# Sums of an LSTM's input blocks moved ahead of the other stream on GpSimd, and the copies of three-token blocks dropped

## The chip, the cores and the metric

The kernel runs on one core of a Trainium2 chip. The metric is the device time of one execution in microseconds (us), the median over several runs. In the profile PE is TensorE's matrix multiplication, PEld its loading of weights, DVE is VectorE, ACT is ScalarE, POOL is GpSimd, and SP is SyncE, from which most DMAs are issued. "L1154" is line 1154 of the kernel's source.

## The reference

Four residual layers work on x of shape 128 x 64 x 256 (batch, tokens, channels), in fp32, each on a layer-normalized and rectified input: a graph convolution with batch normalization, a graph network with LSTMs, attention over the graph, and attention with four heads. The change lies in the second layer. There h, after two graph convolutions, goes through four LSTMs one after the other:

```python
for p in range(1, MAX_SKIP + 1):
    nw = Tv // p
    wins = h[:, :nw * p, :].reshape(Bv * nw, p, Hd)
    last = _lstm_last(Wih[p - 1], Whh[p - 1], bih[p - 1], bhh[p - 1], wins)
    idx = jnp.arange(nw) * p + (p - 1)
    h = h.at[:, idx, :].set(last.reshape(Bv, nw, Hd))
```

LSTM p takes windows of p tokens, runs p steps with its own weights (`g = x_t @ Wih.T + h @ Whh.T + bias`, gates i, f, g, o from zero states) and writes the last state over the last token of each window. LSTM p + 1 reads the result. With 64 tokens there are 64, 32, 21 and 16 windows per batch entry for p = 1, 2, 3, 4.

## The kernel before

The batch is cut into 16 chunks of 512 rows (8 batch entries of 64 tokens). Layer 2 takes two chunks at a time in eight passes, numbered 0 to 7. A pass holds h in a tile `hT`, channels on the partitions in two halves k, and in the free dimension token t and batch entry b (16 of them). An LSTM of p tokens thus has nw x 16 columns: 1024, 512, 336 and 256.

**Seven products instead of eight.** The product of a gate's weights with a step's columns is taken as a product of 2 x 2 blocks: two halves of the channels by two halves of the columns. It is done with seven block products, numbered 1 to 7, in place of eight. Products 1, 2 and 3 take blocks of the tokens as they are. Products 5, 6, 7 and 4 take sums of blocks, which `differences` makes in four subtractions (L313, L314, L315, L316): t1 = b12 − b11, t3 = b22 − b12, t2 = b22 − t1, t4 = b21 − t2. For the input part x these sums are made on GpSimd into the tile `xd`, a pool of two buffers; for the state part h they are made on VectorE into `hd`. Products of x and h add up in the same PSUM bank; the pool has two banks each of the tags x, y and z.

**Three tokens.** The columns are cut in halves by window for p = 2 and 4, so that a block is rows of 16 contiguous values. 21 windows are odd, so for p = 3 the cut is by batch entry: a block is 21 rows of 8 values. In that case `operands_x` (L1086) also copies the blocks of products 1, 2 and 3 into `xd` (L1097), three copies of 128 x 168 on GpSimd for each step but the first, behind the four sums.

**One LSTM's start** (`lstm`, L1026): `operands_x(1)` is the first thing it emits. The first step has no state; its 12 products g (L1125) read `hT` directly into the six banks (two with tag y for gate i, two with z for gate g, two with x for gate o), and ScalarE makes the gates from them (`first_acts`, L1112), freeing the banks in the order y, z, x. Then, before the state of the first step is there, come the x parts of the second step's products 5 (bank y), 3 and 2 (bank z), L1154. The state h and its sums follow on VectorE, and then the rest of the products. At the last step `new_state` writes into `hT` (L1079, L1083).

**The single-token LSTM** (`single`, L1278) has its whole work in seven products of 512 columns with three gates each (L1308). It makes its sums at its own start for passes 1 to 7, the first (t1) on VectorE and the other three on GpSimd. In pass 0 it makes them after its first yield.

**The other stream.** The LSTMs are generators, and at each of their yields, numbered n = 0 to 21 in a pass, the kernel emits pieces of other work, given by lists of places such as `CONV`, `BEGUN`, `RESIDUAL` and `AHEAD`: the graph convolutions of the next pass, the way back of the previous pass's result, and the normalization ahead of layer 3. The order in which all this is emitted is the order on each engine's queue. An LSTM yields a last time at its end: n = 3, 7, 13 and 21 for p = 1 to 4. Pieces that stand there are emitted before the next LSTM's `operands_x(1)`. At n = 3 and n = 7 these are layer-norm statistics: four pairs of bn_stats and bn_aggr on VectorE (L159, L160), then the reciprocal root rstd on GpSimd (`rsqrt`, L99 and L100), which waits for them. Of those at n = 3 the scale and shift follow at n = 4 (nmr, L194, on VectorE; four applications on ScalarE, L196), ahead of that LSTM's first gates on ScalarE. Only in pass 0 does n = 21 have a piece of VectorE's, the addition of line 284.

Of the kernel before, what the change touches and what calls it, by code (L numbers as in the profile page):

```python
# [8 lines left out]
F32 = mybir.dt.float32  # L9
# [4 lines left out]
P = 128  # L14
# [5 lines left out]
def kernel(  # L20
# [22 lines left out]
    nc = tc.nc  # L43
    B, T, D = x.shape
    H0 = w1t.shape[1]
    KD = D // P
# [3 lines left out]
    SKIP = wih_t.shape[0]  # L50
    HEADS = 4
    HD = D // HEADS
    CH = 512
    NJ = CH // P
    NB = CH // T
    NCH = B * T // CH
    SUP = 2
# [11 lines left out]
    def pool(name, bufs, side="left"):  # L69


        stack = ExitStack()
        return stack.enter_context(tc.tile_pool(name=name, bufs=bufs, side=side,
                                                reuse_waits="tile")), stack.close
# [234 lines left out]
    def differences(engine, dst, b11, b12, b21, b22, third=None):  # L309


        t1, t2, t3, t4 = dst
        return [lambda: engine.tensor_tensor(t1, b12, b11, OP.subtract),  # L313
                lambda: ((third or engine).tensor_tensor(t3, b22, b12, OP.subtract),  # L314
                         engine.tensor_tensor(t2, b22, t1, OP.subtract)),  # L315
                lambda: engine.tensor_tensor(t4, b21, t2, OP.subtract)]  # L316
# [272 lines left out]
    with tc.manual_schedule(engines={mybir.EngineType.PE, mybir.EngineType.DVE,  # L589
# [27 lines left out]
        for c in range(2, NCH - 1):  # L617
            a, z = sevens[c], sevens.get(c - 1)
# [3 lines left out]
            b = sevens[c + 1] = Seven1(c + 1) if c + 1 < NCH - 1 else None  # L622
# [142 lines left out]
    with tc.manual_schedule(engines={mybir.EngineType.PE, mybir.EngineType.DVE,  # L765
# [3 lines left out]
        for c in range(2, NCH - 1):  # L769
            a, b, z = sevens[c], sevens.get(c + 1), sevens.get(c - 1)  # L770
# [80 lines left out]
    l1, close_l1 = pool("l1", 2)  # L851
# [31 lines left out]
    def load_sets(n):  # L883
        for _ in range(min(n, len(coming))):
            p, q = coming.pop(0)
            wsets[p, q] = w1.tile([P, 15, P], F32, tag="wset", name=f"wset_{p}_{q}", bufs=6)
            nc.sync.dma_start(wsets[p, q], wfar[p, q])
# [4 lines left out]
    hTs = {}  # L892
# [130 lines left out]

    BLOCKS = {1: (0, 8), 2: (2, 9), 3: (7, 14), 4: (3, 10), 5: (4, 11), 6: (5, 12), 7: (6, 13)}

    def lstm(p, hv, name, follows):  # L1026


        nb = hv.shape[3]
        nw = hv.shape[2] // p  # L1030
        n = nb * nw
        m = n // 2
        bs = bias[:, p - 1, :]
        odd = nw % 2
        inner = nb // 2 if odd else nb

        def cols(s):
            return slice(s, s + (nw - 1) * p + 1, p)

        def tokens(k, s, j):  # L1040
            v = hv[:, k, cols(s), :]
            if odd:
                return v[:, :, j * inner : (j + 1) * inner]
            return v[:, j * nw // 2 : (j + 1) * nw // 2, :]

        def folded(t):
            return t.rearrange("p (a b) -> p a b", b=inner)
# [35 lines left out]
                engine.tensor_tensor(tokens(c, s, j), folded(gate(3, c, part)),  # L1083
                                     folded(gate(2, c, part)), OP.mult)

        def operands_x(s):  # L1086

            t = l1.tile([P, 7 * (T // 3) * NB], F32, tag="xd", name=f"xd_{name}_{s}", bufs=2)
            t = [folded(t[:, i * m : (i + 1) * m]) for i in range(7 if odd else 4)]
            b = {(k, j): tokens(k, s, j) for k in range(KD) for j in range(2)}  # L1090
            for f in differences(nc.gpsimd, t[:4], b[0, 0], b[0, 1], b[1, 0], b[1, 1]):
                f()
            o = dict(zip((5, 6, 7, 4), t))
            for i, (kind, kj) in enumerate(((1, (0, 0)), (2, (1, 0)), (3, (1, 1)))):
                if odd:

                    nc.gpsimd.tensor_copy(t[4 + i], b[kj])  # L1097
                o[kind] = t[4 + i] if odd else b[kj]
            return o

        b = {(k, j): hn[:, k, halves[j]] for k in range(KD) for j in range(2)}
        dh = differences(nc.vector, [hd[:, i, :m] for i in range(4)], b[0, 0], b[0, 1], b[1, 0], b[1, 1])
        oh = {i: folded(a) for i, a in {1: b[0, 0], 2: b[1, 0], 3: b[1, 1], 4: hd[:, 3, :m],
                                        5: hd[:, 0, :m], 6: hd[:, 1, :m], 7: hd[:, 2, :m]}.items()}
        ox = {1: operands_x(1)}

        banks = {(q, c): bank(f"g{q}_{name}_{c}", tag) for q, tag in ((0, "y"), (2, "z"), (3, "x"))
                 for c in range(KD)}
# [76 lines left out]
        def each(us, *fs):  # L1185
            for f in fs:
                for u in us:
                    f(u)
# [4 lines left out]
        def do(f, *a):  # L1193
            return lambda u: getattr(u, f)(*a)
# [4 lines left out]
        for s in range(1, p):  # L1199
            last = s == p - 1  # L1200
            B = [Unit(q, s) for q in (1, 3)]
            if not last:
                ox[s + 1] = operands_x(s + 1)
            each(A, pe(5, "h"), do("copy", 5), pe(1), do("copy", 1), pe(3, "h"), pe(6, "x"), pe(6, "h"),
                 pe(2, "h"), do("u4"), do("c11"), do("c12"))
            each(B, pe(5), do("copy", 5))
            each(A, do("act", 0), pe(7), do("c22"), do("act", 1))
            each(B[:1], pe(3), pe(2))
            each(A, pe(4), do("act", 2))
            if last:  # L1210
                load_sets(2)
            nc.gpsimd.tensor_mul(gates[:, 0, :, :n], gates[:, 0, :, :n], gates[:, 2, :, :n])  # L1212
            each(B[1:], pe(3), pe(2))
            each(B, pe(1), do("copy", 1))
            yield
            each(B, pe(6))
            A = [] if last else [Unit(q, s + 1) for q in (0, 2)]
            each(A, pe(5, "x"))

            def cell(c, part):  # L1220
                nc.vector.tensor_mul(cells[:, c, part], cells[:, c, part], gate(1, c, part))
                nc.vector.tensor_add(cells[:, c, part], cells[:, c, part], gate(0, c, part))  # L1222
                nc.scalar.activation(gate(2, c, part), cells[:, c, part], AF.Tanh)  # L1223

            if last:

                each(B[:1], do("u4"), do("c11"), pe(7))
                each(B[1:], do("u4"), pe(7))
                each(B[:1], do("c22"), do("c12"), do("act", 0))
                each(B[1:], do("c22"), do("c11"), do("c12"), do("act", 0))  # L1230
                cell(0, every)
            else:
                for u in B:
                    each([u], do("u4"), do("c11"), do("c12"), do("act", 0))
                cell(0, every)
                each(B, pe(7), do("c22"))
            each(B, do("act", 1))
            each(A[:1], pe(3, "x"), pe(2, "x"))
            new_state(s, 0, every)
            if not last:  # L1240
                dh[0]()
            each(A[1:], pe(3, "x"), pe(2, "x"))
            each(B, pe(4))
            B[0].act(2)
            cell(1, halves[1])
            B[1].act(2)
            cell(1, halves[0])
            new_state(s, 1, halves[1])
            if not last:
                dh[1]()  # L1250
            new_state(s, 1, halves[0], nc.gpsimd if follows and last else nc.vector)
            if last:
                load_sets(2)
            else:
                dh[2]()
            yield
# [18 lines left out]

    KINDS1 = {1: 0, 2: 1, 4: 2, 5: 3, 6: 4, 7: 5, 3: 6}

    def single(b, name, begun):  # L1278

        m = CH
        wide = b[0, 0].shape[1:]
# [5 lines left out]
        def folded(a):  # L1289
            return a.rearrange("p (a b) -> p a b", b=wide[1]) if len(wide) > 1 else a  # L1290
# [1 line left out]
        def at(g, c, j):  # L1292
            return (more if j else cells)[:, c, :m] if g == 2 else gates[:, 2 * g + j, c, :m]

        t = []
        for i in range(2):
            part = l1.tile([P, 7 * (T // 3) * NB], F32, tag="xd", name=f"xd_{name}_{i}", bufs=2)
            t += [folded(part[:, a : a + m]) for a in range(0, 2 * m, m)]
        right = {1: b[0, 0], 2: b[1, 0], 3: b[1, 1], 4: t[3], 5: t[0], 6: t[1], 7: t[2]}
        ys, xs_ = [[bank(f"{n}_{name}_{g}", tag) for g, tag in enumerate(tags)]  # L1300
                   for n, tags in (("y1", "yyz"), ("x1", "zxx"))]

# [20 lines left out]
        def state(c, j):  # L1323
            nc.vector.tensor_mul(b[c, j], folded(at(2, c, j)), folded(at(0, c, j)))

        def copy(dst, kind):
            for g in range(3):
                nc.scalar.copy(at(g, *dst), ps(g, kind))
# [2 lines left out]
            for g in range(3):  # L1331
                nc.vector.tensor_add(at(g, *dst), at(g, *dst), ps(g, kind))

        first = differences(nc.vector, t, b[0, 0], b[0, 1], b[1, 0], b[1, 1])[:1]
        rest = differences(nc.gpsimd, t, b[0, 0], b[0, 1], b[1, 0], b[1, 1])[1:]
        if begun:
            for f in first + rest:
                f()
        product(2)
        copy((0, 0), 2)  # L1340
        if not begun:
            yield
            for f in first + rest:
                f()
        product(1)
        add((0, 0), 1)
        for g in range(3):
# [31 lines left out]
        tanh(1, 0)  # L1379
        state(1, 1)  # L1380
        state(1, 0)
        yield

    def lstms(sc, hT):
        hv = hT.rearrange("p k (t b) -> p k t b", t=T)

        def tokens(k, j):
            if sc:
                return hv[:, k, j * T // 2 : (j + 1) * T // 2, :].rearrange("p t b -> p (t b)")
            return hv[:, k, :, j * NB : (j + 1) * NB]  # L1390

        yield from single({(k, j): tokens(k, j) for k in range(KD) for j in range(2)}, f"{sc}_1", sc > 0)
        for p in range(2, SKIP + 1):
            yield from lstm(p, hv, f"{sc}_{p}", p == SKIP and sc < NCH // SUP - 1)

    def new_hT(sc):

# [654 lines left out]
```

## Time and profile before

| | before |
|---|---|
| median of 3 runs | 1901.11 us (1900.84 to 1902.15) |
| span of the profiled execution | 1897.3 us |
| layer 2's LSTM passes in it | about 279 to 1520 us, a middle pass about 157.4 us |
| GpSimd copies of three-token blocks (L1097) | 48, of 0.31 to 0.60 us |
| GpSimd sums, 128 / 168 / 256 / 512 columns | from 0.45 / 0.53 / 0.72 / 1.26 us each |

The table's last two rows are the durations of the instructions themselves[...]. A line of a timeline has the start, the duration, the engine, the source line, the operation, out<-in, the shape, the number of merged instructions, and in brackets how long the engine stood idle before it and which instruction released it. Every TensorE product appears as two matmuls, so that 12 products g are "x24".

### The profile page before, as it was taken

To read this page: it belongs to the slowest core of one execution; us is meant where nothing else is said; L and a number is where in the kernel's file an instruction comes from. 1 tells how busy PE (TensorE), PEld (TensorE's weight loads), DVE (VectorE), ACT (ScalarE), POOL (GpSimd) and SP (SyncE) were. 2 spreads that over 40 slices of the span, in tenths; PEclk is the share of its full clock that TensorE was granted. 3 is DMA by queue.
4 is the path that set the end of the run, shared out by engine and by line. 5 is a ranking of instruction groups with operands and counts; after the bars stand their busy time and mean duration, and the time that the engine had idled before them with its cause. 6 is when DMAs were issued, how large, how long until landed. Compare 5 with 4: busy or idle time off the path is not lost.

```text
span 1897.3 us, 39092 instructions
## 1 busy us (share of the span) xinstructions
PE 1862.9 (98%) x15077; PEld 1478.2 (78%) x15077; DVE 1238.9 (65%) x3150; ACT 1015.9 (54%) x2284; POOL 569.7 (30%) x752
## 2 busy tenths in 40 slices
PE   8999989999999999999999999999999999999998
PEld 6877856895896798689589679868969967777776
DVE  6768746566576666667657666665565567677776
ACT  5766544556456446555645645655565544444453
POOL 5856621212221322222322231222122213233232
PEclk9999999999999999999999999999999999999999
DMA  3223643225334433333433443333144345444433
GB/s 114 78 68 149 232 168 109 72 88 184 106 129 145 144 128 129 113 119 115 150 117 129 150 139 137 130 109 106 54 150 139 103 134 157 135 139 152 143 114 113
DMA packets 111273, 241.45 MB, mean 127 GB/s; under 512 B 11504, under 2 KB 74864, under 8 KB 111088
## 3 DMA queue, kind: packets, MB, share of 16 engines
q1 hardware_dynamic: 110192, 237.09, 37.1%
q8 instruction: 119, 1.95, 0.4%
q0 software_dynamic: 320, 1.05, 0.2%
q10 hardware_dynamic: 576, 0.82, 0.1%
q14 instruction: 66, 0.54, 0.1%
HBM read 170.50 MB, written 68.42 MB: 126 GB/s over the span
## 4 chain that ended last, share of the span: by engine, by line
PE 86%; DVE 7%; POOL 3%; ACT 2%; issue 1%; DMA 0%; DVEq 0%; SPq 0%; ACTq 0%
PE x L1154 22%; PE z L1154 11%; PE g L1125 7%; PE v L1542 6%; PE y L1154 5%; PE x L1308 4%; PE y L1308 3%; PE p_q L1549 3%; PE v L915 3%; PE X L1738 3%; PE X L423 2%; PE X L499 2%; PE u L929 2%; PE Y L1738 1%; PE Y L423 1%
## 5 line engine op out<-in xcount | busy, mean ns | idle before, releaser
L1163 DVE TENSOR_TENSOR gates<-gates,x 128x128 f32<-128x128 f32 (+2 forms) x384 | 118.3, 320 | 332.1 <-PE x L1154 324.9
L1154 PE MATMUL x<-xd,wset 128*128 128x128 f32 (+2 forms) x1280 | 285.6, 311 | 0.7 <-DVE gates L1163 0.2
L1154 PE MATMUL x<-hd,wset 128*128 128x128 f32 (+2 forms) x1152 | 246.7, 303 | 0.0
L1212 POOL TENSOR_TENSOR gates<-gates 128x512 f32<-128x512 f32 (+2 forms) x48 | 74.9, 1560 | 521.7 <-ACT gates L1068 521.7
L1154 PEld LDWEIGHTS x<-xd,wset 128*128 128x128 f32 x1280 | 202.1, 190 | 19.1 <-DVE gates L1163 6.1
L1068 ACT ACTIVATE gates<-gates,bias 128x256 f32<-128x256 f32 (+4 forms) x384 | 170.4, 490 | 56.2 <-DVE gates L1163 52.8
L1154 PEld LDWEIGHTS x<-hd,wset 128*128 128x128 f32 x1152 | 185.1, 191 | 5.0
L1125 PE MATMUL g<-hT,wset 128*128 128x256 f32 (+2 forms) x576 | 183.9, 474 | 1.1 <-DVE hT L1079 1.1
L1160 ACT COPY gates<-y 128x128 f32<-128x128 f32 (+2 forms) x192 | 54.2, 293 | 212.9 <-PE y L1154 212.4
L1125 PEld LDWEIGHTS g<-hT,wset 128*128 128x128 f32 x576 | 108.6, 190 | 69.7 <-issue 38.5
L1154 PE MATMUL z<-hs,wset 128*128 128x128 f32 (+2 forms) x768 | 154.0, 303 | 0.0
L1154 PEld LDWEIGHTS z<-hs,wset 128*128 128x128 f32 x768 | 119.8, 191 | 3.3
L1160 ACT COPY gates<-x 128x128 f32<-128x128 f32 (+2 forms) x192 | 56.4, 295 | 93.7 <-PE x L1154 92.9
L1163 DVE TENSOR_TENSOR gates<-gates,z 128x128 f32<-128x128 f32 (+2 forms) x384 | 104.3, 315 | 0.1
L1068 ACT ACTIVATE gates<-x,bias 128x128 f32<-128x128 f32 (+2 forms) x192 | 74.7, 389 | 49.4 <-PE x L1154 46.5
L1154 PE MATMUL z<-hT,wset 128*128 128x128 f32 (+1 forms) x512 | 97.1, 302 | 0.0
L1112 ACT ACTIVATE gates<-g,bias 128x512 f32<-128x512 f32 (+2 forms) x144 | 74.5, 559 | 32.1 <-PE g L1125 31.6
L1154 PE MATMUL x<-hs,wset 128*128 128x128 f32 (+2 forms) x384 | 84.8, 303 | 0.0
L1223 ACT ACTIVATE gates<-cell 128x256 f32<-128x256 f32 (+2 forms) x144 | 55.2, 384 | 50.5 <-DVE cell L1222 49.0
L1154 PE MATMUL y<-xd,wset 128*128 128x128 f32 (+2 forms) x384 | 77.4, 304 | 3.4 <-ACT gates L1112 3.4
L1154 PE MATMUL y<-hd,wset 128*128 128x128 f32 (+2 forms) x384 | 80.1, 311 | 0.0
L1154 PEld LDWEIGHTS z<-hT,wset 128*128 128x128 f32 x512 | 76.7, 191 | 3.9 <-ACT gates L1112 0.6
(329 smaller groups left out, 4211.5 us busy)
## 6 DMA issues: line engine op xcount, KB each, us to landing
wset<-wfar SPq DMA_DIRECT2D x96, 960.0 KB, 6.6
hT<-far_h SPq DMA_DIRECT2D x124, 128.0 KB, 3.1
far_h<-hm SPq DMA_DIRECT2D x16, 512.0 KB, 3.0
far_n<-xs SPq DMA_DIRECT2D x16, 512.0 KB, 3.3
xs<-far_n SPq DMA_DIRECT2D x64, 128.0 KB, 4.2
far_x<-xs SPq DMA_DIRECT2D x16, 512.0 KB, 3.0
x<-far_x SPq DMA_DIRECT2D x64, 128.0 KB, 3.2
xt<-in_x_dram SPq DMA_DIRECT2D x15, 512.0 KB, 4.1
```

The lines of the kernel that those rows point to most:

```text
L423: nc.tensor.matmul(self.banks[tag][:, i * CH // 2 : (i + 1) * CH // 2], w, self.at[kind], start=first and not i, stop=True, skip_group_che ...
L915: nc.tensor.matmul(banks[m], wg0_sb[:, k, m * P : (m + 1) * P], agg[:, k, :], start=(k == 0), stop=(k == KD - 1))
L1068: nc.scalar.activation(gate(q, c, part), src, AF.Tanh if q == 2 else AF.Sigmoid, bias=bs[:, q * KD + c : q * KD + c + 1])
L1112: nc.scalar.activation(columns_of(gate(q, c)), natural(banks[q, c][:, :n].rearrange("p (w b) -> p w b", b=nb)), AF.Tanh if q == 2 else AF. ...
L1125: nc.tensor.matmul(banks[q, c][:, :n].rearrange("p (w b) -> p w b", b=nb), wsets[p, q][:, 2 * k + c, :], hv[:, k, : (nw - 1) * p + 1 : p, ...
L1154: nc.tensor.matmul(folded(self.psum(kind)), wsets[p, self.q][:, BLOCKS[kind][i], :], (ox[self.s] if part == "x" else oh)[kind], start=firs ...
L1160: nc.scalar.copy(gate(self.q, kind // 5, halves[kind // 5]), self.psum(kind))
L1163: nc.vector.tensor_add(gate(self.q, *dst), gate(self.q, *a), self.psum(kind))
L1212: nc.gpsimd.tensor_mul(gates[:, 0, :, :n], gates[:, 0, :, :n], gates[:, 2, :, :n])
L1308: nc.tensor.matmul(folded(ps(g, kind)), wih1[:, g, KINDS1[kind], :], right[kind], start=kind in (2, 5, 1), stop=True, skip_group_check=True)
L1542: nc.tensor.matmul(ps[:, i, :], hT[:, k, j, :], w[:, k, first : first + D], start=(k == 0), stop=(k == KD - 1))
L1738: nc.tensor.matmul(st[c, tag][:, i * CH // 2 : (i + 1) * CH // 2].rearrange("p (a n) -> p a n", n=P), w, st[c, "o7"][kind], start=first an ...
```

## The change

The sums of an LSTM's input blocks leave the start of `lstm` and `single`. A function `ending`, called at the end of each LSTM just before its last yield, makes those for the next LSTM: `operands_x(p + 1, ..., 1)` for the next p, or `block_sums` of the next pass's tile after p = 4. So they come ahead of whatever the other stream puts at that yield, on GpSimd and, for t1 of the single-token LSTM, on VectorE. The copies for p = 3 are dropped: products 1, 2 and 3 read their blocks in `hT`, as they do for p = 2 and 4. Sums for later steps of an LSTM stay where they were.

The purpose is that the sums start as soon as the tokens they need are written, and that nothing is copied that TensorE can read in place.

```diff
+    def operands_x(p, hv, name, s):
+        nw, nb, inner, tokens = columns_x(p, hv)
+        m = nw * nb // 2
+        t = l1.tile([P, 7 * (T // 3) * NB], F32, tag="xd", name=f"xd_{name}_{s}", bufs=2)
+        t = [t[:, i * m : (i + 1) * m].rearrange("p (a b) -> p a b", b=inner) for i in range(4)]
+        b = {(k, j): tokens(k, s, j) for k in range(KD) for j in range(2)}
+        for f in differences(nc.gpsimd, t, b[0, 0], b[0, 1], b[1, 0], b[1, 1]):
+            f()
+        return {5: t[0], 6: t[1], 7: t[2], 4: t[3], 1: b[0, 0], 2: b[1, 0], 3: b[1, 1]}
...
-            for i, (kind, kj) in enumerate(((1, (0, 0)), (2, (1, 0)), (3, (1, 1)))):
-                if odd:
-
-                    nc.gpsimd.tensor_copy(t[4 + i], b[kj])
-                o[kind] = t[4 + i] if odd else b[kj]
...
-        ox = {1: operands_x(1)}
+        ox = {1: x1}
...
             if last:
                 load_sets(2)
+                ending()
...
-        if begun:
-            for f in first + rest:
-                f()
         product(2)
         copy((0, 0), 2)
+        begun = bool(t)
         if not begun:
             yield
-            for f in first + rest:
-                f()
+            t = block_sums(b, name)
...
+        def ending(p):
+
+            if p < SKIP:
+                operands[p + 1] = operands_x(p + 1, hv, names[p + 1], 1)
+            elif sc < NCH // SUP - 1:
+                nxt = hTs[sc + 1].rearrange("p k (t b) -> p k t b", t=T)
+                operands[1] = block_sums(blocks(sc + 1, nxt), f"{sc + 1}_1")
```

More of the change, by code (lines that the diff above doesn't have):

```diff
@@ L1024, with columns_x, tokens, lstm @@
     BLOCKS = {1: (0, 8), 2: (2, 9), 3: (7, 14), 4: (3, 10), 5: (4, 11), 6: (5, 12), 7: (6, 13)}
-    def lstm(p, hv, name, follows):
-        nb = hv.shape[3]
-        nw = hv.shape[2] // p
+    def columns_x(p, hv):
+        nw, nb = hv.shape[2] // p, hv.shape[3]
+        odd = nw % 2
+        inner = nb // 2 if odd else nb
+        def tokens(k, s, j):
+            v = hv[:, k, s : s + (nw - 1) * p + 1 : p, :]
+            if odd:
+                return v[:, :, j * inner : (j + 1) * inner]
+            return v[:, j * nw // 2 : (j + 1) * nw // 2, :]
+        return nw, nb, inner, tokens
+    def operands_x(p, hv, name, s):
[7 more added lines that the diff above has]
+        return {5: t[0], 6: t[1], 7: t[2], 4: t[3], 1: b[0, 0], 2: b[1, 0], 3: b[1, 1]}
+    def lstm(p, hv, name, follows, x1, ending):
+        nw, nb, inner, tokens = columns_x(p, hv)
         n = nb * nw
@@ L1034, in lstm @@
         odd = nw % 2
-        inner = nb // 2 if odd else nb
         def cols(s):
             return slice(s, s + (nw - 1) * p + 1, p)
-        def tokens(k, s, j):
-            v = hv[:, k, cols(s), :]
-            if odd:
-                return v[:, :, j * inner : (j + 1) * inner]
-            return v[:, j * nw // 2 : (j + 1) * nw // 2, :]
         def folded(t):
@@ L1084, in new_state @@
                                      folded(gate(2, c, part)), OP.mult)
[L1086 to L1091, printed above, removed]
-                f()
-            o = dict(zip((5, 6, 7, 4), t))
-            for i, (kind, kj) in enumerate(((1, (0, 0)), (2, (1, 0)), (3, (1, 1)))):
-                if odd:
-                    nc.gpsimd.tensor_copy(t[4 + i], b[kj])
-                o[kind] = t[4 + i] if odd else b[kj]
-            return o
         b = {(k, j): hn[:, k, halves[j]] for k in range(KD) for j in range(2)}
@@ L1202, in lstm @@
             if not last:
-                ox[s + 1] = operands_x(s + 1)
+                ox[s + 1] = operands_x(p, hv, name, s + 1)
             each(A, pe(5, "h"), do("copy", 5), pe(1), do("copy", 1), pe(3, "h"), pe(6, "x"), pe(6, "h"),
@@ L1276, with blocks, tokens, block_sums @@
     KINDS1 = {1: 0, 2: 1, 4: 2, 5: 3, 6: 4, 7: 5, 3: 6}
-    def single(b, name, begun):
+    def blocks(sc, hv):
+        def tokens(k, j):
+            if sc:
+                return hv[:, k, j * T // 2 : (j + 1) * T // 2, :].rearrange("p t b -> p (t b)")
+            return hv[:, k, :, j * NB : (j + 1) * NB]
+        return {(k, j): tokens(k, j) for k in range(KD) for j in range(2)}
+    def block_sums(b, name):
+        t = []
+        for i in range(2):
+            part = l1.tile([P, 7 * (T // 3) * NB], F32, tag="xd", name=f"xd_{name}_{i}", bufs=2)
+            for a in range(0, 2 * CH, CH):
+                v = part[:, a : a + CH]
+                wide = b[0, 0].shape[1:]
+                t.append(v.rearrange("p (a b) -> p a b", b=wide[1]) if len(wide) > 1 else v)
+        a = b[0, 0], b[0, 1], b[1, 0], b[1, 1]
+        for f in differences(nc.vector, t, *a)[:1] + differences(nc.gpsimd, t, *a)[1:]:
+            f()
+        return t
+    def single(b, name, t, ending):
         m = CH
@@ L1293, in at @@
             return (more if j else cells)[:, c, :m] if g == 2 else gates[:, 2 * g + j, c, :m]
[L1295 to L1299, printed above, removed]
+        right = {1: b[0, 0], 2: b[1, 0], 3: b[1, 1]}
         ys, xs_ = [[bank(f"{n}_{name}_{g}", tag) for g, tag in enumerate(tags)]
@@ L1332, in add @@
                 nc.vector.tensor_add(at(g, *dst), at(g, *dst), ps(g, kind))
-        first = differences(nc.vector, t, b[0, 0], b[0, 1], b[1, 0], b[1, 1])[:1]
-        rest = differences(nc.gpsimd, t, b[0, 0], b[0, 1], b[1, 0], b[1, 1])[1:]
-        if begun:
-            for f in first + rest:
-                f()
         product(2)
         copy((0, 0), 2)
+        begun = bool(t)
         if not begun:
             yield
-            for f in first + rest:
-                f()
+            t = block_sums(b, name)
+        right.update(zip((5, 6, 7, 4), t))
         product(1)
@@ L1381, in single @@
         state(1, 0)
+        ending()
         yield
+    operands = {}
     def lstms(sc, hT):
         hv = hT.rearrange("p k (t b) -> p k t b", t=T)
[L1387 to L1392, printed above, removed]
+        names = [f"{sc}_{p}" for p in range(SKIP + 1)]
+        def ending(p):
[4 more added lines that the diff above has]
+                operands[1] = block_sums(blocks(sc + 1, nxt), f"{sc + 1}_1")
+        yield from single(blocks(sc, hv), names[1], operands.pop(1, None), lambda: ending(1))
         for p in range(2, SKIP + 1):
-            yield from lstm(p, hv, f"{sc}_{p}", p == SKIP and sc < NCH // SUP - 1)
+            yield from lstm(p, hv, names[p], p == SKIP and sc < NCH // SUP - 1, operands.pop(p),
+                            lambda: ending(p))
     def new_hT(sc):
```

## The prediction

> **What bounds the kernel now.** I read the page first, then TensorE's own waits, then the order of time around them.
>
> ```profile
> span 1897.3 us, 39092 instructions
> PE 1862.9 (98%) x15077; PEld 1478.2 (78%) x15077; DVE 1238.9 (65%) x3150; ACT 1015.9 (54%) x2284; POOL 569.7 (30%) x752
> ...
> PE 86%; DVE 7%; POOL 3%; ACT 2%; issue 1%; DMA 0%; DVEq 0%; SPq 0%; ACTq 0%
> ```
>
> TensorE is busy 98% of the span, so work taken from GpSimd brings nothing by itself; only the moments at which TensorE stands still count. The view of its waits lists them:
>
> ```profile
> PE z L1154 <- POOL xd L1097: 9.5, 6, 1.7
> PE y L1154 <- ACT gates L1112: 3.4, 3, 2.3
> ...
> PE y L1308 <- DVE xd L313: 0.9, 1, 0.9
> ```
>
> (total us, times, longest.) The longest total is a wait for the copies of line 1097, exactly what the change deletes: six times, 1.7 us at most. Six suggests once in most of the eight passes. The order of time at the start of the three-token LSTM of pass 2, TensorE first (weight loads apart; start, duration), then GpSimd:
>
> ```profile
> 653.85 6.94 PE L1125 MATMUL g<-hT,wset 128*128 128x336 f32 x24
> 660.62 0.73 PE L1154 MATMUL y<-xd,wset 128*128 128x168 f32 x4
> 662.91 1.27 PE L1154 MATMUL z<-xd,wset 128*128 128x168 f32 x7 [1.55 <-POOL xd L1097]
> ```
>
> ```profile
> 657.51 0.23 POOL L99 TENSOR_SCALAR rstd_n<-mv_n 128x4 f32<-128x4 f32 x1 [12.65 <-DVE mv_n L160]
> 657.82 1.04 POOL L100 TENSOR_TENSOR rstd_n<-rstd_n,mhalf 128x4 f32<-128x4 f32 x1
> 658.83 0.54 POOL L313 TENSOR_TENSOR xd<-hT 128x168 f32<-128x168 f32 x1
> 659.33 0.54 POOL L314 TENSOR_TENSOR xd<-hT 128x168 f32<-128x168 f32 x1
> 659.82 0.81 POOL L315 TENSOR_TENSOR xd<-hT,xd 128x168 f32<-128x168 f32 x1
> 660.71 0.68 POOL L316 TENSOR_TENSOR xd<-hT,xd 128x168 f32<-128x168 f32 x1
> 661.34 1.52 POOL L1097 COPY xd<-hT 128x168 f32<-128x168 f32 x3
> ```
>
> VectorE's last write of hT (L1083) runs from 654.86 to 655.28: there the tokens are complete, but GpSimd takes up the other stream's rstd first, and that waits for four statistics on VectorE until 657.5. Sums and copies follow only then. The products y start at 660.62. Four of 168 columns pass at 0.285 us a pair (at 666.02 and 666.30 pairs start 0.28 apart), so the next could start at 661.19; it starts at 662.91. TensorE loses 1.72 us. The same spacing of starts, measured at all eight three-token LSTMs, gives 1.71, 1.72, 1.86, 1.72, 1.72 and 1.72 us in passes 1 to 6: 10.45 us. Pass 0 loses 0.1 there. In pass 7 no rstd stands ahead on GpSimd, the copies are done at 1441.2, and the z products follow y by 0.57 us (1442.81, 1443.38), the bare pace: the trace already holds one LSTM without this wait.
>
> [...] The trace agrees (pairs of 0.45 us start every 0.285), so I count starts. [...] a GpSimd sum of 256 columns takes 0.73 us beside the PSUM copy of line 1005 and 1.27 beside the addition of line 284. [...] In pass 0 the single-token LSTM already reads hT in runs of 8: six products of 512 columns take 2.57 us from one group's start to the next (285.36 to 287.94), as they do from xd (280.21 to 282.79).
>
> **The change part by part.**
>
> *Copies removed*: 6 for each of eight passes, 48 in all, at 0.31 to 0.60 us on GpSimd (line 1097's rows). The z products then need only hT, complete at 655.28, and their banks, which ScalarE's first four gates free at 658.00 + 2.23 = 660.23. TensorE comes at 661.19. So the whole 1.72 us goes: −10.4 us in six passes.
>
> *Does the next wait take it back?* TensorE then reaches y<-hd at 663.6 instead of 665.34. Its hd (VectorE L313) was done at 662.14, the last hs at 662.67, the difference for product 6 at 663.63 while TensorE would ask for it near 666.6; the aggregation between needs a tile that VectorE finished at 658.6. Every one is ready at least 1 us early. Nothing.
>
> *Sums ahead of the other stream*: no instruction is added; on GpSimd the four sums change places with rstd at the ends of the one- and two-token LSTMs. For three tokens: sums from 655.3, 4 x 0.5 = 2.0 us beside one-input statistics, done at 657.4 as rstd's input comes (657.5). Nobody is delayed. Alone this would also have removed the wait: copies of 0.3 each would end at 658.4. The two parts therefore share one gain; it is not counted twice.
>
> *The same for two tokens* is where a new wait could arise, because there the rstd is wanted at once:
>
> ```profile
> 619.11 2.07 ACT L196 ACTIVATE cv<-xs,nmr_b,rstd_b 128x256 f32<-128x256 f32 x4 [4.15 <-DVE nmr_b L194]
> 621.09 1.24 ACT L1112 ACTIVATE gates<-g,bias 128x512 f32<-128x512 f32 x2
> ```
>
> ScalarE applies the other stream's normalization, then makes the first gates; TensorE takes the y banks at 622.78. Tokens are complete at 614.77. Four sums of 256 columns take 4 x 0.70 = 2.8 us alone, 3.9 if two are slowed as in this trace. So rstd starts at 617.7 to 618.8 instead of 617.00 and ends 1.35 later (617.00 to 617.31 + 1.04), at 619.05 to 620.1. nmr waits for it on VectorE; behind nmr is queued the addition of line 284, and ScalarE's four applications wait, then the first gates that free the y banks. Before, nmr ran at 618.93, held by VectorE's copies until 619.0, so ScalarE comes 0.2 to 1.2 us later. The first y bank is free after one gate, at 621.09 + 0.66 = 621.75, 1.0 us before TensorE takes it, the second with 0.8 to spare. I take the lower value, since VectorE runs one-input statistics in that time: no wait. The upper end costs 0.4 us in six passes, 2.4 us.
>
> *Pass 0, two tokens*: here TensorE already waits 2.3 us on those first gates. The sums now start beside the addition of line 284, slow each other, and rstd comes 0.3 to 0.6 later: +0.4 us.
>
> *Single-token sums, pass 0 to 1*: only here another unit stands ahead on VectorE (the addition of line 284, 437.50 to 439.0, and t1 at 438.98, slowed to 1.75 us). Now t1 is first: the 0.9 us wait of y L1308 goes; by starts 1.0. In later passes nothing changes places: 0.
>
> *Strided reads*: 192 products of three tokens now read hT in runs of 8, at 0 by the comparison above. Two semaphores at some x products (GpSimd besides VectorE or ScalarE): both long past, 0.
>
> Sum: −10.4 − 1.0 + 0.4 = −11.0; 1901.1 − 11.0 = 1890.1.
>
> **The rivals.**
>
> B. *The late rstd bites.* ScalarE is held for 1.2 us in six passes, TensorE for 0.4, and pass 0 loses more: 1890.1 + 3 = 1893. For it: the slack is only 0.8 us. Against it: VectorE's statistics leave GpSimd alone.
>
> C. *A wait in place of the one removed*: TensorE comes 1.7 us early to y<-hd or a bank that is not ready, and the gain shrinks to that of the single sums: about 1900. For it: there are many such waits at hundredths of a us. Against it: pass 7 runs without the wait, and nothing stops behind it (y<-hd at 1445.61 comes straight after the filling transposes).
>
> D. *Strided reads slow TensorE.* The 192 products are recorded as 384 matmuls of 0.142 us, 54.5 us. Half as slow again: +27, so 1890.1 + 27 = 1917, slower than before. For it: no product in the trace yet reads runs of 8 that lie three tokens apart. Against it: pass 0's runs of 8 at full pace, and the first products g read hT of three tokens in place, in runs of 16, 336 columns at 0.283 us.
>
> E. *More than counted*: fewer GpSimd operations beside VectorE's shorten its chains, and some of the gaps of about 0.1 us ahead of x<-xd at 168 columns go (by the spacing of starts 53 of them, 5.3 us in all): half of them, 1887.5.
>
> **How the numbers follow.** Forecast 0.68, B 0.17, C 0.07, D 0.05, E 0.03. Time: the forecast's, 1890.1. Range: from E, 1887.5, to B with its upper cost in pass 0 and a part of the gain lost, 1896; C and D, 0.12, are left out. Faster: forecast, B and E, 0.88. Same: C, 0.07. Slower: D, 0.05.
>
> **What would show it.** Right: no z wait for xd on TensorE, z<-hT 0.57 us after y in all passes, y L1308 without its wait, p=3 groups at 168 columns with the mean of 0.306 us and the pace unchanged. B: PE y waiting for ACT gates L1112 near 622 in six passes. C: y<-hd waiting for DVE. D: z<-hT of 168 columns spaced wider than 0.142. The sum is wrong if the span of a middle pass (157.4 us) does not fall by about 1.7.

## The result, and the profile after

| | before | after |
|---|---|---|
| median | 1901.21 us (1900.84 to 1902.15) | 1890.13 us (1889.59 to 1892.57) |
| ratio, with its 95% interval | | 0.9943 (0.9926 to 0.9961) |
| profiled execution, span | 1897.3 us | 1890.8 us |

The change saves 11.1 us by the medians; the interval of the ratio allows 7.4 to 14.1. The page of the changed kernel (first lines, then the chain that ended last by engine):

```profile
span 1890.8 us, 39088 instructions
PE 1863.0 (99%) x15077; PEld 1479.3 (78%) x15077; DVE 1236.6 (65%) x3150; ACT 1016.6 (54%) x2284; POOL 551.4 (29%) x704
...
PE 90%; DVE 5%; ACT 2%; issue 1%; POOL 1%; DMA 1%; SPq 0%; DVEq 0%; ACTq 0%
```

TensorE does the same 15077 matmuls in a span 6.5 us shorter; GpSimd has 48 instructions fewer and has nearly left the chain (3% before, 1% now). The view of TensorE's waits (total us, times, longest), its first lines:

```profile
PE y L1155 <- ACT gates L1113: 3.3, 2, 2.5
PE idle_a L151 <- POOL ident masks.py:199: 2.7, 1, 2.7
PE s L1843 <- issue: 2.3, 2, 1.2
```

The 9.5 us of z waiting for the copies and the 0.9 us of the single-token y waiting for t1 stand nowhere in it. What leads now is pass 0's old wait for the first gates, and a line that hardly counted before (0.4 us): attention products at which TensorE waited for "issue", nothing that the profile names. The start of the three-token LSTM of pass 2, first TensorE in order of time, then GpSimd:

```profile
653.31 6.94 PE L1126 MATMUL g<-hT,wset 128*128 128x336 f32 x24
660.09 0.73 PE L1155 MATMUL y<-xd,wset 128*128 128x168 f32 x4
660.66 1.30 PE L1155 MATMUL z<-hT,wset 128*128 128x168 f32 x8
```

```profile
652.35 0.59 POOL L313 TENSOR_TENSOR xd<-hT 128x168 f32<-128x168 f32 x1 [8.01 <-DVE hT L1095]
655.06 0.55 POOL L314 TENSOR_TENSOR xd<-hT 128x168 f32<-128x168 f32 x1 [2.12 <-DVE hT L1099]
655.56 0.54 POOL L315 TENSOR_TENSOR xd<-hT,xd 128x168 f32<-128x168 f32 x1
656.18 0.54 POOL L316 TENSOR_TENSOR xd<-hT,xd 128x168 f32<-128x168 f32 x1
657.21 0.23 POOL L99 TENSOR_SCALAR rstd_n<-mv_n 128x4 f32<-128x4 f32 x1 [0.49 <-DVE mv_n L160]
```

The z products start 0.57 us behind the y products (before: 2.29). The sums are done at 656.7, when before they had not begun, and the other stream's rstd still waits for its statistics, not for them.

Where the time went, by stages cut at TensorE's own starts: "passes" runs from the first single-token product (y<-hT) to the start of the last x<-hd product, "behind them" from there to the end of the span. "Stops" counts the waits for "issue" of about half a us or more behind the passes at those attention products and one p_q, by the spacing of starts.

| kernel, profiled execution | passes, us | behind them, us | stops |
|---|---|---|---|
| before | 1252.4 | 371.2 | 1 |
| after | 1242.1 | 374.5 | 3 |

The passes gave 10.3 us, the rest took 3.3 back, and the passes begin 0.5 us later (at 274.2 against 273.7 us). So the spans differ by 6.5 us and the times of the two profiled executions by 6.9 (1899.42 and 1892.57), the medians by 11.1. The passes of "after" also hold a stretch at half TensorE clock, which two of the experiments take up.

### The profile page after: what moved, and what is told of

Same layout as the page of the kernel before. It is cut to its first block, busy times and chain, and to the rows that moved or that the text cites. A ratio compares the mean times of both kernels' runs of the same rounds, so it can differ in the third digit from the quotient of the medians.

```text
span 1890.8 us, 39088 instructions
## 1 busy us (share of the span) xinstructions
PE 1863.0 (99%) x15077; PEld 1479.3 (78%) x15077; DVE 1236.6 (65%) x3150; ACT 1016.6 (54%) x2284; POOL 551.4 (29%) x704
## 3 DMA queue, kind: packets, MB, share of 16 engines
q8 instruction: 119, 1.95, 0.4%
## 4 chain that ended last, share of the span: by engine, by line
PE 90%; DVE 5%; ACT 2%; issue 1%; POOL 1%; DMA 1%; SPq 0%; DVEq 0%; ACTq 0%
PE x L1155 23%; PE z L1155 11%; PE g L1126 9%; PE y L1155 6%; PE v L1568 6%; PE x L1329 4%; PE y L1329 3%; PE u L929 3%; PE p_q L1575 3%; PE v L915 3%; PE X L1764 3%; PE X L423 2%; PE X L499 2%; PE Y L1764 1%; PE Y L423 1%
## 5 line engine op out<-in xcount | busy, mean ns | idle before, releaser
L1155 PE MATMUL x<-xd,wset 128*128 128x128 f32 (+2 forms) x1152 | 256.8, 311 | 0.7 <-DVE gates L1164 0.2
L1155 PEld LDWEIGHTS x<-xd,wset 128*128 128x128 f32 x1152 | 180.8, 190 | 19.0 <-DVE gates L1164 6.1
L1155 PE MATMUL z<-hT,wset 128*128 128x128 f32 (+2 forms) x768 | 148.4, 306 | 0.0
L1155 PEld LDWEIGHTS z<-hT,wset 128*128 128x128 f32 x768 | 117.9, 192 | 4.4 <-ACT gates L1113 0.5
L1155 PE MATMUL x<-hT,wset 128*128 128x128 f32 (+2 forms) x384 | 85.7, 305 | 0.4 <-ACT gates L1084 0.2
```

Of the source, the lines that this page charges most:

```text
L1155: nc.tensor.matmul(folded(self.psum(kind)), wsets[p, self.q][:, BLOCKS[kind][i], :], (ox[self.s] if part == "x" else oh)[kind], start=firs ...
```

## The experiments

**Which part makes the gain?** The forecast said that dropping the copies and moving the sums share one gain. Two kernels do one part each. First, the kernel before with the copies alone dropped:

```diff
-            t = [folded(t[:, i * m : (i + 1) * m]) for i in range(7 if odd else 4)]
+            t = [folded(t[:, i * m : (i + 1) * m]) for i in range(4)]
...
-                if odd:
-
-                    nc.gpsimd.tensor_copy(t[4 + i], b[kj])
-                o[kind] = t[4 + i] if odd else b[kj]
+                o[kind] = b[kj]
```

> The kernel before, with the three-token copies dropped and nothing else: the sums stay at each LSTM's start, behind the other stream. Theory (the two parts share one gain, the copies' wait): the z wait for xd is gone in passes 1 to 6, 10.4 us, and the y L1308 wait of 0.9 us stays: about 1890.7, 0.9945 of before. Rival (the gain comes from the early sums; a late xd stops the next product instead): y<-xd or a later x product then waits for the sums, and most of the gain is missing: 1898 to 1901.

Measured: 1893.05 us, ratio 0.9960 (0.9945 to 0.9975), 2.3 above the expected 1890.7. In its order of time z follows y by 0.57 us with the sums still behind the rstd:

```profile
659.23 0.73 PE L1151 MATMUL y<-xd,wset 128*128 128x168 f32 x4
659.80 1.30 PE L1151 MATMUL z<-hT,wset 128*128 128x168 f32 x8
```

The single-token wait (y for DVE xd L313, 0.9 us, once) is still there. Second, the changed kernel with the 48 copies put back behind the early sums:

```diff
+        o = dict(zip((5, 6, 7, 4), t))
+        for i, (kind, kj) in enumerate(((1, (0, 0)), (2, (1, 0)), (3, (1, 1)))):
+            if nw % 2:
+                nc.gpsimd.tensor_copy(t[4 + i], b[kj])
+            o[kind] = t[4 + i] if nw % 2 else b[kj]
+        return o
```

> The changed kernel with the 48 copies put back behind the sums. Theory: with the sums ahead of rstd the copies end near 658.4 on the clock of pass 2, before TensorE asks at 661.2, so nothing is lost: 1890, equal to the changed kernel within 1 us, no z wait for xd. Rival (the copies as such cost): GpSimd's 18 us more show, or rstd comes 0.9 us later for three tokens and something waits: 1893 to 1900.

Measured: 1890.41 us, ratio 0.9945 (0.9930 to 0.9960). No z wait either; in its order of time on GpSimd the copies are done at 656.1, 3.1 us ahead of the z products that read them (659.21), and the rstd comes right behind them:

```profile
655.20 0.86 POOL L1051 COPY xd<-hT 128x168 f32<-128x168 f32 x3
656.03 0.23 POOL L99 TENSOR_SCALAR rstd_n<-mv_n 128x4 f32<-128x4 f32 x1
```

Either part alone takes away all six waits; the gain is shared, as forecast. To tell the first kernel from the whole change, both were run again side by side, without an edit.

> The changed kernel once more, on the chip of the other runs. The run with the copies dropped alone came out at 1893.05 us where the LSTM passes of its trace are 0.6 to 1.1 us longer than with early sums. Theory (what is beyond that lies in stops of TensorE for its own instructions after the LSTM passes, which differ from one execution to the next): 1890 to 1892, three or fewer such stops, not the same as in the first trace. Rival (the stops belong to the program): the same three stops of 1.1 to 1.3 us at the same instructions.

> The kernel before with only the copies dropped, once more. Theory of the early sums being worth the 1.0 us wait of the single-token LSTM and no more: 1 us above the changed kernel of the same call. Rival: 2.5 to 3 us above it again, so that the early sums shorten something else.

Measured: changed 1890.91 us, ratio 0.9946 (0.9934 to 0.9959); copies dropped alone 1891.86, ratio 0.9950 (0.9937 to 0.9964). The difference of 0.95 us is the size of the single-token wait; the intervals overlap, so the wait in the trace carries this more than the times do. Moreover the three stops lie at the same places in both executions of the changed kernel (109.7, 267.4 and 351.5 us behind the passes, then 109.1, 266.8 and 350.7): they belong to the program, not to chance.

**The single-token sums alone.** The changed kernel, with pass 1's block sums made at that LSTM's start:

```diff
-            elif sc < NCH // SUP - 1:
+            elif 0 < sc < NCH // SUP - 1:
...
+        if sc == 1:
+            operands[1] = block_sums(blocks(sc, hv), names[1])
```

> The changed kernel with the single-token sums of pass 1 made at that LSTM's start, behind the addition of line 284, as before. Theory: the y L1329 wait of 1.0 us is back, everything else as in the changed kernel: +1.0 us, 1891. Rival (this sum was never on the path): 1890.

Measured: 1892.45 us, ratio 0.9954 (0.9942 to 0.9967), 1.5 us above the changed kernel that ran beside it. The intervals overlap, so here too the trace carries more than the times; the line comes back in its view of waits:

```profile
PE y L1329 <- DVE xd L313: 0.9, 1, 0.9
```

**Pass 0's two-token LSTM.** The forecast gave 0.4 us here for a later rstd, and in the profiled execution of the changed kernel TensorE falls to half clock just behind its stand there, the wait for the first gates. This kernel makes these sums late again, in pass 0 alone:

```diff
-        ox = {1: x1}
+        ox = {1: x1 or operands_x(p, hv, name, 1)}
...
-            if p < SKIP:
+            if sc == 0 and p == 1:
+                operands[2] = None
+            elif p < SKIP:
```

> The changed kernel, but in pass 0 the two-token sums are made at that LSTM's start, behind the other stream, as before. The profile of the changed kernel shows there a stand of TensorE of 2.5 us (before: 2.3) and, just after it, a granted clock of 0.5 for 3.4 us, which costs 1.7 us. Theory (the longer stand brings on the lower clock): stand back at 2.3, no lower clock, at most 1889.5. Rival (the lower clock is chance): the same time as the changed kernel, and the lower clock comes or not in either.

Measured: 1890.78 us, ratio 0.9948 (0.9931 to 0.9964). The stand did not shrink: 2.74 us by starts, against 2.67 in the changed kernel and 2.48 before. And there is no half clock. The theory that the longer stand alone brings it falls. The windows around the stand (window; its length; busy time and count of PE, PEld, DVE, ACT, POOL; granted clock; DMA share; GB/s), first the profiled execution of the changed kernel, then its second one:

```profile
304.00:307.00 3.00, 0.50 (x2) 0.03 (x1) 0.18 (x2) 2.79 (x6) 0.00 (x0) 1.00 0.43 175
307.00:309.00 2.00, 2.00 (x7) 1.25 (x8) 0.96 (x2) 1.81 (x4) 0.00 (x0) 0.82 0.44 145
309.00:311.00 2.00, 2.00 (x6) 1.57 (x5) 1.29 (x3) 2.00 (x4) 0.00 (x0) 0.50 0.96 150
311.00:313.00 2.00, 2.00 (x67) 1.36 (x66) 1.93 (x5) 0.07 (x1) 0.00 (x0) 0.82 0.68 230
```

```profile
309.00:311.00 2.00, 2.00 (x35) 1.51 (x38) 1.33 (x3) 1.81 (x5) 0.00 (x0) 1.00 0.96 155
```

Same program, same stand, 0.50 in one execution and 1.00 in the other. The passes of the first are 1.5 us longer (1242.1 and 1240.6 us).

**How near is the late rstd (rival B)?** To measure the slack, the fourth two-token sum is made five times instead of once in passes 1 to 6, with the same values each time:

```diff
-                operands[p + 1] = operands_x(p + 1, hv, names[p + 1], 1)
+                o = operands[p + 1] = operands_x(p + 1, hv, names[p + 1], 1)
+                for _ in range(4 if p == 1 and 0 < sc < NCH // SUP - 1 else 0):
+                    nc.gpsimd.tensor_tensor(o[4], o[2], o[6], OP.subtract)
```

> The changed kernel, with the fourth two-token sum made five times instead of once in passes 1 to 6, so that rstd starts about 2.1 us later there (output unchanged). Theory (ScalarE's normalization stands ahead of the first gates, with 0.8 to 1.0 us to spare): TensorE's y<-xd waits for ACT gates L1113 about 1.0 us in each of six passes: +6 us, 1896. Rival (the slack is wider or the gates don't wait for rstd): no such wait, 1890. Second rival (GpSimd's contention slows VectorE's chain): more than +10.

Measured: 1903.60 us, ratio 1.0013 (1.0005 to 1.0020): 13 us on top of the changed kernel. One line each from its view of waits and, in pass 2, its order of time on VectorE and on TensorE:

```profile
PE y L1155 <- ACT gates L1113: 11.1, 8, 2.5
```

```profile
622.46 0.16 DVE L194 SCALAR_TENSOR_TENSOR nmr_b<-mv_b,rstd_b 128x4 f32<-128x4 f32 x1 [2.24 <-POOL rstd_b L100]
```

```profile
625.45 1.18 PE L1155 MATMUL y<-xd,wset 128*128 128x256 f32 x4 [1.29 <-ACT gates L1113]
```

In the changed kernel the same nmr and the same products y stand here:

```profile
618.39 0.15 DVE L194 SCALAR_TENSOR_TENSOR nmr_b<-mv_b,rstd_b 128x4 f32<-128x4 f32 x1
```

```profile
622.25 1.03 PE L1155 MATMUL y<-xd,wset 128*128 128x256 f32 x4
```

Rival B's mechanism exists and looks exactly so. With this kernel shifted by 1.74 us against the changed one (it comes to the products g at 612.40, the changed one at 610.66), nmr is 622.46 − 1.74 − 618.39 = 2.33 us later, and the first y bank costs 1.45: a slack of 0.9 us, where the forecast read 1.0. The penalty was larger than the expected 6 us: the first y bank alone waits 1.45 us in each of six passes in place of 1.0, and the second y bank and z wait too. The passes of this trace are 11.2 us longer than those of the changed kernel's first one (1253.3 and 1242.1 us, each with one stretch at half clock). The second rival's mark, more than 10 us, was thereby passed, but its cause is not seen: the copies of line 1005 on VectorE take 1.29 us for two in both kernels, and nmr waits for the rstd.

**Can pass 0's remaining waits be moved away?** The lists of places of the first pass and of the last one were changed, so that some of the other stream's pieces, the applications ahead of pass 0's first gates among them, stand one yield later:

```diff
-    FIRST = (1, 3, 3, 4, 4, 5, 6, 7, 8, 9, 10, 11, 12, 12), (3, 6, 7, 8, 10, 13, 14, 15, 16, 17, 18, 19, 20, 20)
+    FIRST = (1, 3, 3, 5, 5, 6, 7, 8, 9, 10, 11, 12, 13, 13), (3, 6, 7, 9, 10, 13, 14, 15, 16, 17, 18, 19, 20, 20)
-    FINAL = (4, 5, 10, 12, 12, 14), (6, 7, 11, 14, 14, 16)
+    FINAL = (4, 5, 10, 12, 12, 14), (6, 7, 11, 15, 15, 16)
```

> The changed kernel with the pieces of the other stream that hold up first gates moved one yield on: FIRST[0] from its fourth piece on (4, 4, 5, ... become 5, 5, 6, ...), FIRST[1]'s fourth piece from 8 to 9, FINAL[1]'s fourth and fifth from 14 to 15. Theory (what is left of TensorE's longer stands in the LSTM passes is ScalarE applying a normalization ahead of the first gates): y<-xd loses its waits of 2.7, 0.7 and 1.0 us: 4.4 us less, about 1886, and no lower clock after the first of them. Rival (the pieces only move: their aggregation, or hd, then stops TensorE instead): less than 2 us gained, 1888 to 1891.

Measured: 1901.87 us, ratio 1.0004 (0.9995 to 1.0012). Its view of waits:

```profile
PE agg_b L214 <- ACT hT L940: 4.9, 2, 4.5
PE x L1155 <- ACT gates L1161: 4.5, 3, 1.9
PE s L1843 <- issue: 2.8, 3, 1.1
PE idle_a L151 <- POOL ident masks.py:199: 2.7, 1, 2.7
PE g L1126 <- DVE hT L1095: 2.7, 3, 2.2
PE x L1155 <- DVE gates L1164: 1.6, 2, 1.4
```

The 3.3 us of y are gone, and more than 10 us of others stand in their place. The rival had the mechanism: the pieces only move, and other products wait for them instead. It did not have the size, since it expected 1888 to 1891 and the kernel is 11 us slower than the changed one. Its trace also holds 13.7 us at half clock, 10.2 of them in the passes; how much of the 11 us is theirs was not separated.

**The stops behind the passes.** The kernel with copies put back has one stop, the changed kernel three, though nothing behind the passes was touched. Two kernels with copies were profiled a second time: the kernel before, and the one with early sums and copies.

> The kernel before once more, one look. Theory (TensorE's stops for its own instructions after the LSTM passes belong to the program): as in its first trace one stop, 131 us after the last product of the LSTM passes, and none near 110, 267 and 351 us; 371.2 us from that product to the end, where the changed kernel has 373.7 to 374.5. Rival (they differ from one execution to the next): other places or a time of 373 to 374.5.

> The changed kernel with the 48 copies put back, once more, one look. Same question: its first trace has one stop, at 131 us, and 371.8 us to the end. Theory (belongs to the program): the same. Rival: other places.

Measured: 1901.67 and 1889.03 us, one execution each. Both again have one stop, at 131.7 us behind the passes, and 371.8 us from the end of the passes to the end of the span. So every kernel with the copies so far takes some 371 to 372 us there, and every one without them 373 to 375 us. Two things go with the copies. GpSimd has 48 instructions more, and TensorE has 24 fewer: without copies, the trace has 24 more semaphore waits, for VectorE or ScalarE, as instructions of their own, three in each of the eight three-token LSTMs. The page shows the sum: 39088 instructions after, 39112 with copies put back; from the second to the first, −48 + 24. The next kernel gives GpSimd its 48 instructions back, as copies of 128 x 8 that nobody reads:

```diff
+        whole = t
...
+        for i, kj in enumerate(((0, 0), (1, 0), (1, 1)) if nw % 2 else ()):
+            nc.gpsimd.tensor_copy(whole[:, (4 + i) * m : (4 + i) * m + inner], b[kj][:, 0])
```

> The changed kernel with 48 copies of 128x8 that nobody reads, where the copies of 128x168 stood: as many instructions on GpSimd as before, but a third of their time or less. Theory (TensorE's stops for instructions are tied to how many instructions the program has on the engines): one stop at 131 us, about 372 us to the end, and a time of 1888 to 1890. Rival (they are tied to something else): three stops, 374 us, 1890 to 1891.

Measured: 1892.09 us, ratio 0.9950 (0.9934 to 0.9967); three stops (109.4, 266.8, 350.7), 373.8 us behind the passes. It isn't GpSimd's count. The last kernel keeps the copies and gives TensorE 24 instructions more, ahead of the passes (the filling transposes run from 248.1 to 251.0 us): 12 more of them, each a weight load and a matmul.

```diff
-            for at, fill, name in ((6, 16, "d"), (9, 6, "e"), (10, 6, "f")):
+            for at, fill, name in ((6, 28, "d"), (9, 6, "e"), (10, 6, "f")):
```

> The kernel with early sums and copies, with 12 more idle transposes (24 TensorE instructions) put into the fill ahead of the LSTM passes, where TensorE waits anyway. That makes its TensorE stream as long as the changed kernel's (15574 entries on TensorE's queue in the trace, where the kernels with copies have 15550). Theory (after the LSTM passes TensorE stops where its own instructions are not there yet, and the 24 added semaphore waits of the changed kernel moved those places): three stops near 110, 267 and 351 us after the last product of the passes, and 373.5 to 374.5 us from it to the end. Rival (something else in the kernels with copies decides): one stop at 131 us and 371.8 us.

Measured: 1892.08 us, ratio 0.9955 (0.9938 to 0.9971); three stops (109.7, 267.1, 351.3), 374.35 us behind the passes, 2.6 more than without the 24. One place in order of time on TensorE, in the changed kernel, in the one with early sums and copies, and in that with 24 instructions more:

```profile
1623.68 1.11 PE L1843 MATMUL s<-qk 64*64 64x64 f32 x62
1625.93 0.27 PE L1843 MATMUL s<-qk 64*64 64x64 f32 x2 [1.14 <-issue]
```

```profile
1622.24 1.11 PE L1848 MATMUL s<-qk 64*64 64x64 f32 x64
1623.29 1.99 PE L1573 MATMUL v<-w_sb,hT 128*128 128x256 f32 x8
```

```profile
1622.34 1.11 PE L1848 MATMUL s<-qk 64*64 64x64 f32 x62
1624.59 0.27 PE L1848 MATMUL s<-qk 64*64 64x64 f32 x2 [1.14 <-issue]
```

The group of 64 matmuls breaks after the 62nd where TensorE's program has 30651 instructions (counted in the traces), with copies or without, and does not where it has 30627. The number of instructions ahead on TensorE places these stops. (The expectation's 15574 was meant as the queue's entries; the trace has 15562 and 12 matmuls more, the same total.)

Why just there? The profile's page gives a DMA queue of the kind "instruction" (q8, 119 packets, 1.95 MB, every packet 16384 bytes). Between the starts of its first and its last packet TensorE starts 30234 instructions in the trace of before and 30257 in that of after, 256.2 and 256.4 to a packet. By my estimate from these numbers q8 carries TensorE's program, 256 instructions to a packet. Counted from the start of TensorE's trace, all 34 stops behind the passes in the 14 traces come 193 to 196 instructions beyond a multiple of 256, and TensorE goes on 1.2 to 1.7 us after the packet next in turn has landed. At the other 1618 such places the packet next in turn had landed 1.8 us ahead or earlier, and TensorE does not stop. So the stops and the late packets of q8 go together, and 24 instructions more shift which products stand at such a place. That TensorE waits for the packet is read from the traces; no run changed the fetching itself.

## Why the prediction was right

The forecast was 1890.1 us, and 1890.13 came, but that nearness is luck: executions of one kernel spread over some 3 us (1899.60 to 1902.43 for 17 of the kernel before), and terms were off in both directions.

*Copies removed, −10.4*: held. By the spacing of starts, the z<-xd products of 168 columns stood 10.59 us in all before (10.45 of it in passes 1 to 6) and stand 0 after, and the experiments show either part alone doing it.

*The next wait takes back nothing*: held. y<-hd follows at 662.99 with nothing before it, and the spacing of a middle pass falls from 157.4 to 155.6 us, by 1.8 where the forecast asked for about 1.7.

*The same for two tokens, no wait*: the outcome held, the reason only in part. I let the sums begin when the last token is written; in the trace t1 begins as soon as its channel half is written (609.75 in pass 2) and the next sum at 613.46, so two of the four are done by then (614.19). What I had not seen is the other side: VectorE's last write of hT then runs beside a sum and takes 1.19 us in place of 0.69. That VectorE's statistics leave the sums alone, which the forecast took for granted, is shown after the change: where bn_stats runs beside them, 21 sums of 168 columns take 0.53 to 0.55 us and 7 of 256 columns 0.73, and with little or nothing of VectorE's beside them 0.54 to 0.55 and 0.73. The rstd in the end waits for the statistics, as the order of time on GpSimd shows:

```profile
615.40 0.73 POOL L316 TENSOR_TENSOR xd<-hT,xd 128x256 f32<-128x256 f32 x1
616.96 0.23 POOL L99 TENSOR_SCALAR rstd_b<-mv_b 128x4 f32<-128x4 f32 x1 [0.83 <-DVE mv_b L160]
```

*Pass 0, +0.4*: +0.2 at the two-token stand (2.48 to 2.67) and +0.2 at the three-token LSTM, which I had not counted. The late variant shows that the two-token part is within what the stand varies by.

*Single-token sums, −1.0*: held; 1.04 to 0 by starts, and the wait came back when they were moved back.

*Strided reads, 0*: held. The z<-hT products of 168 columns run at 1.30 us for 8 in the order of time, and by starts at 0.142 us each, as when they read the copies.

Undisturbed by the half clock, the passes fall from 1252.4 to 1240.6 us, by 11.8 where the sum said 11.0. Most of the 0.8 is a second stand, of 0.1 us, at the next z product behind each of the six waits, which went with them (starts 0.247 us apart in place of 0.142) and which the sum left out. Rival E's gaps of about 0.1 us ahead of the x products did not go: 5.2 us in all before and after. The step that failed is the last clause, "Two semaphores at some x products ... both long past, 0". They are long past as waits; but they are 24 instructions, and with those the stretch behind the passes takes some 2 to 3 us more in every trace. That term should have been +2 to +3.

Compared like with like, the change seems worth less than the medians say. The executions of before and after that both hold a stretch at half clock differ by 9.1 us (1901.67 and 1892.57), those that both lack it by 8.7 (1899.42 and 1890.71), and the stages of the latter pair give much the same: 11.8 off the passes and 2.5 onto the rest. These are single executions. If the kernel before met the stretch more often than the changed one did, the medians' 11.1 (10.6 when it was run again, 1901.50 and 1890.91) would follow; executions without a trace can't show it, so this stays open.

What else stays open. Why those few packets of q8 come late isn't shown. Nor do the medians show the stops clearly: early sums with copies, one stop, have 1890.41, the change, three stops, 1890.13; only the kernel with 24 instructions more lies 1.7 us above its neighbour, in another group of runs and with intervals that overlap.

## What to carry to other kernels

Where an engine with slack holds up the bounding one, look at what stands ahead on its queue: dropping the last item and moving the whole group ahead of a waiting instruction can each pay the same gain once, so they aren't added up. Work put ahead of a shared chain needs its slack measured, not only read; here it was 0.9 us, and 3.2 us more of sums in each of six passes cost about 2 us in each. And count what an operand's new source adds to the program of the bounding engine itself: a wait that is long past costs no waiting, but it is an instruction, and there were 24 of them here.

## What the runs showed of the hardware

24 instructions more or less on TensorE, hundreds of us earlier (the last experiment's near 250 us, its first stop at 1624), decide between one stop and three behind the passes, of 0.4 to 1.2 us each. At each of the 34 stops in the 14 traces the packet of 16384 bytes next in turn on q8 had landed 1.2 to 1.7 us before TensorE went on; at the other 1618 such places it was 1.8 us or more.

The stretches at half clock (granted 0.50), apart from the one that runs to the end of each trace, last 3.413 us (6.827 once) and begin at whole multiples of 3.413 us behind the first clock record (at 300.373 us, 88 of them, in one trace), in every kernel that has them. Behind pass 0's stand of 2.4 to 2.8 us they came in some executions (2.37 us with the copies dropped) and not in others (2.74 us with pass 0's sums late). Where the stand falls on that grid tells the two apart in these traces: at pass 0's stand the half clock came in the five where TensorE was busy for only 0.75 to 1.60 us of one period of the grid (1.29 in the first execution of the changed kernel), just behind that period, and in none of the eight where it was busy for 1.7 us or more of each (1.75 at the least in the first execution of the kernel before). It is no general threshold, since three stretches ahead of the passes follow 2.0 to 2.3 us of busy time, and no run moved a stand on purpose.
